# Five edits to a graph-network and feed-forward kernel: float16 counts, Gelus inside the attention, later source rows, other PSUM places, weight loads by another queue

## The chip, the cores and the metric

The kernel runs on one core of one Trainium2 chip. The metric is the device time of one execution in microseconds (us). Engines are named as the profile names them: PE (TensorE; PEld is its weight load), DVE (VectorE), ACT (ScalarE), POOL (GpSimd) and SP (SyncE, which here only issues DMAs). The sequencer of POOL issues DMAs too.

## The reference, cut to what matters

Four residual layers over 1250 nodes with 1024 features, and 20000 edges sorted by destination:

```
edge_index = stack([src, dst])
x = x + L0_gnn(layernorm(x), W, a_l, a_r, src, dst)     # attention over edges, 4 heads of 256
x = x + L0_ffn(layernorm(x), rail_maker, rail_up, w_cproj)   # small rails, exact gelu, @ w_cproj.T (16384 -> 1024)
x = x + L1_gnn(layernorm(x), edge_index, W, b)          # (x W.T + b), then a normalized sum over neighbours and self
x = x + L1_ffn(layernorm(x), shared + one of 8 experts by argmax)
```

In the attention, `e = leaky_relu(el[src] + er[dst])`, a softmax over the edges of each destination, and a sum of `alpha * z[src]`. The kernel turns the edge list into a dense matrix of counts (how often source n meets destination m), so that both graph layers become dense matrix products: the attention weight of a pair is its count times an exponential.

## The kernel before, in words

The nodes are cut into T = 10 tiles of R = 125. One function, gnn_ffn_kernel, writes all instructions; a scheduler orders those of each engine by their place in the program and by when their inputs are ready in its own model. `tc.issue_after(ins)` adds an edge: what the block issues on the engine of `ins` comes behind `ins`.

**Counts, L243 to L407.** The edges lie in 160 chunks of 125. For each chunk DVE makes two one-hot matrices in float16 (low_hot L286, place_hot L291), and PE multiplies them into counts in PSUM (count, L343). keep_counts (L297) copies a tile's counts to SBUF by ACT in float32 (cn) and stores them in DRAM (cnt_d) by SP. mark (L307) makes a table of -1e30 where a count is zero, for the search of the largest score. turn_counts (L312) transposes ten blocks of 125 x 125 per tile on PE (L318), and ACT copies them as int16 into CT (L321, L324). Beside it, a tile of x is normalized and transposed (L159), and z_tile (L232) makes Z for heads 0 and 1 (L228), copies it by ACT (L235) and sums el and er by DVE (L239). A fallback in tc.If counts all chunks when an edge lies outside its window; it does not run with these inputs.

**Second half of Z, L467 to L488.** For j = 0 to 19 heads 2 and 3 get their Z tiles. Beside it DVE searches the largest scores (maxima, L424), at j = 10 el_row(2) transposes head 2's el (L183), stores it to DRAM and spreads it to all partitions (L187, L192, both POOL DMAs), at j = 14 bounds makes the rows of heads 0 and 1, and at j = 16 the first three weights of head 0 are made ahead of that j's z_tile.

**Attention, L549 to L641.** attend(h, b) runs for four heads and two halves of the destinations. For each of ten source tiles weight (L455) makes an operand w: DVE (L458), ACT Exp (L459), DVE (L461, times the counts). PE adds w times Z into five PSUM accumulators po (L559). The last two source tiles are taken together, accumulator by accumulator. Then ACT copies the sums of the weights (L567), DVE inverts them (L568, in a group of two and a group of three) and adds to X (L571). Generators passed as `between` issue other work after each weight: the search for head 3 (els3, whose el_row stands ahead of the first attend) or first_half, which normalizes and transposes five tiles. After the last attend eight products of the rail matrices (hidden_rows, L541, four at a time over 32 rows) go through two PSUM buffers `pt` to ACT's Gelu (L639), and make the first blocks Y of the large product.

**Large product, L652 to L948.** The 16384 x 1024 product is cut into NB = 16 blocks of 49 steps (15 of seven by seven Strassen-like products, the last of another form). projection_plan (L54) writes the order of steps, and at which step each sum of X blocks (weights) and Y blocks (Gelu outputs) is issued to DVE (add_up, L721). A step is eight L728 matmul instructions; accumulate (L734) copies the result by ACT into one of five buffers (L737), and POOL sends it to DRAM with an adding DMA (L741); `sent` holds the last one. SP loads weights (load_weights, L516). In blocks 2 to 5 the GCN weights are prepared: at step 24 load_quarters (L751) issues four loads of 256 KB to four places taken from the free list of Y blocks, and at step 31 sum_quarters (L757) makes four sums on DVE (L759 to L762) behind the last add_up issued, and SP stores them (L764). Steps 28 and 30 hold the rails of the next block (L536).

**GCN product and aggregation, L950 to L1160.** linear (L975) multiplies by the prepared weights, the last result read from PSUM by L1030. Then Hs is split into a rounded part Hr (ACT, L1089) and the rest (DVE, L1091), and gather (L1105) multiplies each tile's counts with both (L1108) into PSUM tiles ph. load_counts (L1003) reads counts from cnt_d by POOL's queue into a float32r tile. logits uses PSUM tile pg, turn uses pt. The experts' layer (L1171 on) is not touched.

Of the kernel before, what the change touches and what calls it, by code (L numbers as in the profile page):

```python
# [102 lines left out]
def gnn_ffn_kernel(ctx, tc, x, src, dst, gat_w, a_l, a_r, maker, up, cproj,  # L103
# [14 lines left out]
    cnt_d = dram.tile([GS, R, LO], F32, name="cnt_d")  # L118
    cnt_t = cnt_d.rearrange("g m l -> (g m l)").rearrange("(c p t j) -> t p c j", c=T, p=R, t=T)
# [11 lines left out]
    make_identity(nc, ident)  # L131
    ones_row = const.tile([1, R], F32, name="ones_row")
# [75 lines left out]
    with tc.tile_pool(name="gw", bufs=1) as gwp, tc.tile_pool(name="gps", bufs=3, space=PSUM) as psp:  # L208
# [34 lines left out]
        with tc.tile_pool(name="cc", bufs=1) as ccp, tc.tile_pool(name="cw", bufs=2) as cwp:  # L243
# [10 lines left out]
            near = [[g for g in range(GS) if c in win[g]] for c in range(EC)]  # L254
            limit = ccp.tile([EP, EC], F32, name="limit")
# [41 lines left out]
            def keep_counts(d, parts):  # L297
                cn = cns[d] = cwp.tile([R, HI, LO], F32, name="cn")
                g0 = 0
                for i, pc in enumerate(parts):  # L300
                    n = pc.shape[-1] // LO
                    nc.scalar.activation(cn[:, g0:g0 + n].rearrange("p g l -> p (g l)"), pc, AF.Copy,
                                         accum_out=got[:, d, i % 3:i % 3 + 1])
                    g0 += n
                dma(nc.sync, cnt_d[d * HI:d * HI + HI].rearrange("g m l -> m g l"), cn)
# [6 lines left out]
            def turn_counts(d):  # L312
                cn = cns[d]
                CTv = CT.rearrange("p (h a) n -> p a h n", a=2)
                for blocks in ([(g, 0) for g in range(4)], [(g, 1) for g in range(4)], [(4, 0), (4, 1)]):
                    pt = psp.tile([R, 4, R], F32, name="pt")
                    for i, (g, a) in enumerate(blocks):
                        nc.tensor.transpose(pt[:, i, :], cn[:, g, a * R:(a + 1) * R], ident[:R, :R])  # L318
                    d0 = d * R + blocks[0][0] * GD
                    if len(blocks) == 4:  # L320
                        nc.scalar.copy(CTv[:, a, :, d0:d0 + 4 * GD],  # L321
                                       pt.rearrange("p g m -> p (g m)").rearrange("p (q h) -> p h q", h=HI))
# [69 lines left out]
            with tc.If(elsewhere > 0):  # L392
                with tc.tile_pool(name="hot2", bufs=1) as hotp:
                    for d in range(T):
# [11 lines left out]
                        keep_counts(d, parts)  # L406
# [48 lines left out]
        def weight(h, b, s):  # L455
# [3 lines left out]
            nc.scalar.activation(u, u, AF.Exp, bias=el2[:, h, s:s + 1])  # L459
# [5 lines left out]
        weighed = []  # L465

        with tc.tile_pool(name="mx0", bufs=1) as mxp:  # L467
            search = maxima({h: els0[:, h, :] for h in range(2)}, mxp)
            for j in range(2 * T):
                h, t = 2 + j // T, j % T  # L470
                if j == T:
# [5 lines left out]
                for _ in range(1 + j % 2 if j < T + 4 else 2):  # L477
                    next(search, None)
                if j == T + 6:
                    first_weights = [weight(0, 0, s) for s in range(3)]  # L480
                z_copied, z_summed = z_tile((h,), t, z_first[j][0] if j < 2 else None)
# [67 lines left out]
    with tc.tile_pool(name="aps", bufs=6, space=PSUM) as aps, tc.tile_pool(name="tps0", bufs=2, space=PSUM) as tps:  # L549

        def attend(h, b, between=iter(())):
# [963 lines left out]
```

## Time and profile before

| | us |
|---|---|
| runs: median (lowest, highest) | 2720.31 (2719.29, 2721.19) |
| profiled execution | 2725.58 |
| its span | 2723.9 |
| PE busy in the span | 2690.3 |
| DVE busy | 1662.9 |
| counts stage and first Z half | 0 to about 152 |
| second Z half | 152 to 230 |
| attention | 230 to 413 |
| large product | 419 to about 2210 |
| aggregation | 2350 to about 2462 |

A line of the list of waits has the engine, the tile and line that waited, the releaser, the total in us, how often, and the longest. A line of a stretch has its length, then busy us of PE, PEld, DVE, ACT and POOL with instruction counts, the TensorE clock that was granted (1.00 is full speed), the mean busy share of the 16 DMA engines and GB/s. A line of the timeline has start, duration, engine, line, operation, out<-in, shape, the number of instructions merged, and in brackets the idle time before it with its releaser. SPq and POOLq are the DMA issues of those engines. A matmul of float32 data is two instructions.

### The profile page before, as it was taken

What the parts mean: (1) busy time and instruction counts of PE and PEld (TensorE: products, weight loads), DVE (VectorE), ACT (ScalarE), POOL (GpSimd) and SP (SyncE); (2) the same over time, 40 slices, a digit from 0 to 9 for tenths busy, and PEclk for the clock granted to TensorE, in tenths of its full rate; (3) what the DMA queues carried; (4) which work ended last, traced back from release to release, by engine and by line L of the source; (5) the groups of instructions that cost most, each with busy time, mean ns of one, the idle gap of its engine ahead of it and who ended that gap; (6) DMA issues with size and microseconds to landing.
All of it is one profiled execution on the core that took longest, in us unless ns stands there. A gap on an engine that the chain in (4) does not pass through costs nothing. (4 is left out here: it accounts for less than half of the span.)

```text
span 2723.9 us, 32531 instructions
## 1 busy us (share of the span) xinstructions
PE 2690.3 (99%) x11285; PEld 1906.2 (70%) x11285; DVE 1662.9 (61%) x2884; ACT 949.3 (35%) x1689; POOL 765.8 (28%) x952
## 2 busy tenths in 40 slices
PE   8999999999999999999999999999999999999998
PEld 5678886676666766667667666676676764575797
DVE  9668988564656645655556465564655765532655
ACT  2333445434334343343443433434433011211232
POOL 2000001243333333433333333343333110012253
PEclk9999999999999999999999999999999999999999
DMA  6337216499999999999999999999999570342695
GB/s 188 93 85 182 71 39 220 165 199 164 222 195 184 233 175 194 187 163 204 179 172 201 162 195 182 167 202 172 157 211 268 151 126 12 74 91 85 217 291 170
DMA packets 267609, 452.63 MB, mean 166 GB/s; under 512 B 53382, under 2 KB 143662, under 8 KB 267053
## 3 DMA queue, kind: packets, MB, share of 16 engines
q0 software_dynamic: 126896, 278.80, 59.5%
q1 hardware_dynamic: 140532, 171.55, 21.0%
q8 instruction: 97, 1.59, 0.2%
q14 instruction: 84, 0.69, 0.1%
HBM read 180.57 MB, written 271.90 MB: 166 GB/s over the span
## 5 line engine op out<-in xcount | busy, mean ns | idle before, releaser
L741 POOL DMA_DIRECT2D acc_d<-low x686 | 590.4, 861 | 958.3 <-ACT low L737 907.1
L737 ACT COPY low<-po 128x626 f32<-128x626 f32 x735 | 501.1, 682 | 952.1 <-PE po L728 891.5
L728 PE MATMUL po<-X,arena 128*128 128x313 f32 x2200 | 619.0, 429 | 4.9 <-DVE X L721 4.9
L728 PEld LDWEIGHTS po<-X,arena 128*128 128x128 f32 x2200 | 414.9, 190 | 180.6 <-ACT low L737 16.0
L728 PE MATMUL po<-low,arena 128*128 128x313 f32 x1528 | 431.6, 428 | 0.0
L728 PEld LDWEIGHTS po<-low,arena 128*128 128x128 f32 x1528 | 287.1, 189 | 122.0 <-ACT low L737 11.6
L728 PE MATMUL po<-X,first_w 128*128 128x313 f32 x760 | 216.7, 428 | 0.0
L728 PE MATMUL po<-X,BZ 128*128 128x313 f32 x744 | 214.7, 432 | 0.0
L728 PEld LDWEIGHTS po<-X,first_w 128*128 128x128 f32 x760 | 142.6, 189 | 61.5 <-ACT low L737 7.6
L728 PEld LDWEIGHTS po<-X,BZ 128*128 128x128 f32 x744 | 141.3, 192 | 60.6 <-ACT low L737 5.8
L728 PE MATMUL po<-low,first_w 128*128 128x313 f32 x608 | 173.2, 427 | 0.0
L728 PEld LDWEIGHTS po<-low,first_w 128*128 128x128 f32 x608 | 114.5, 189 | 48.5 <-ACT low L737 4.4
L721 DVE TENSOR_TENSOR X<-X 128x626 f32<-128x626 f32 x125 | 100.4, 808 | 74.6 <-PE po L728 66.0
L228 PE MATMUL pz<-W,xT 128*125 128x256 f32 (+1 forms) x480 | 140.6, 451 | 0.9 <-ACT Z L235 0.6
L728 PE MATMUL po<-low,BZ 128*128 128x313 f32 x488 | 140.1, 427 | 0.0
L721 DVE TENSOR_TENSOR arena<-arena 128x512 f32<-128x512 f32 x126 | 86.5, 688 | 68.4 <-PE po L728 65.9
L721 DVE TENSOR_TENSOR X<-X,low 128x626 f32<-128x626 f32 x106 | 85.2, 807 | 56.6 <-PE po L728 46.4
L228 PEld LDWEIGHTS pz<-W,xT 128*125 128x125 f32 x480 | 88.7, 187 | 44.2 <-issue 33.8
L728 PEld LDWEIGHTS po<-low,BZ 128*128 128x128 f32 x488 | 91.5, 189 | 38.6 <-ACT low L737 3.7
L721 DVE TENSOR_TENSOR X<-low,X 128x626 f32<-128x626 f32 x100 | 80.2, 807 | 54.0 <-PE po L728 49.3
L713 ACT ACTIVATE X<-pz 128x626 f32<-128x626 f32 (+8 forms) x222 | 102.1, 523 | 18.3 <-PE pz L541 18.3
L721 DVE TENSOR_TENSOR low<-X 128x626 f32<-128x626 f32 x99 | 79.7, 808 | 38.3 <-PE po L728 31.1
(346 smaller groups left out, 3540.8 us busy)
## 6 DMA issues: line engine op xcount, KB each, us to landing
acc_d<-low POOLq DMA_DIRECT2D x735, 313.0 KB, 6.2
arena<-in_cproj SPq DMA_DIRECT2D x148, 256.0 KB
xT<-in_w SPq DMA_DIRECT2D x16, 1024.0 KB
BZ<-in_cproj SPq DMA_DIRECT2D x56, 256.0 KB
first_w<-in_cproj SPq DMA_DIRECT2D x52, 256.0 KB
w3t<-in_w SPq DMA_DIRECT2D x8, 1024.0 KB
low<-acc_d SPq DMA_DIRECT2D x20, 313.0 KB
X<-acc_d SPq DMA_DIRECT2D x18, 313.0 KB
```

What stands on the lines that cost most here:

```text
L228: made_z = nc.tensor.matmul(pz, xT[:, k, t * R:(t + 1) * R], W[hs[0] // 2][:, k, i:i + len(hs)], start=(k == 0), stop=(k == KD - 1))
L713: nc.scalar.activation(view(key)[:, :, n0 - n * NQ:n1 - n * NQ], pz[:, 2 * i:2 * i + 2, a + n0 - c0:a + n1 - c0], AF.Gelu)
L721: summed[:] = [tt(view(k), *a, op=ALU.add if sign == "+" else ALU.subtract).ins]
L728: nc.tensor.matmul(po[:, o, :NQ], view(x)[:, q, o * P:(o + 1) * P], view(y)[:, q, :], start=(i == q == 0), stop=(i + 1 == len(pairs) and q ...
L737: nc.scalar.copy(part, po[:, :, :NQ])
L741: sent[:] = [nc.gpsimd.dma_start(out=acc_d[p - 1, i - 1], in_=part, accum_op=ALU.add).ins]
```

## The change

- Counts are kept in float16 in SBUF and DRAM (keep_counts, mark, turn_counts, load_counts); the transposes of counts have float16 operands and output, with an identity of their own. In the fallback the old kind is kept and stored in a second DRAM tensor, all_d, as well.
- In the second half of Z, el_row(2) is issued one j later, and the first three weights come behind the z_tile of their j, with their ACT instructions behind that tile's copy.
- el_row(3) becomes a generator that the first attend runs after its third weight.
- The eight rail products and their Gelus are issued by a generator, in four pieces, inside the last source tiles of the last attend, with the Gelus behind the last Exp; that attend groups its accumulators three and two.
- The four GCN quarter loads go by POOL's queue, behind the last accumulation sent.
- PSUM tiles pg and pt of the aggregation are allocated ahead of ph, so that all three lie in other places.

```diff
+    cnt_d, all_d = (dram.tile([GS, R, LO], f, name=n) for f, n in ((F16, "cnt_d"), (F32, "all_d")))
...
+    ident16 = const.tile([R, R], F16, name="ident16")
+    nc.vector.tensor_copy(ident16, ident[:R, :R])
...
-            def keep_counts(d, parts):
-                cn = cns[d] = cwp.tile([R, HI, LO], F32, name="cn")
+            def keep_counts(d, parts, kind=F16):
+                cn = cns[d] = cwp.tile([R, HI, LO], kind, name="cn" if kind == F16 else "cn32")
...
             def turn_counts(d):
                 cn = cns[d]
+                i16 = cn.dtype == F16
...
                     pt = psp.tile([R, 4, R], F32, name="pt")
+                    pt = pt.rearrange("p g m -> p (g m)").bitcast(F16)[:, :4 * P].rearrange("p (g m) -> p g m", g=4)[:, :, :R] if i16 else pt
                     for i, (g, a) in enumerate(blocks):
-                        nc.tensor.transpose(pt[:, i, :], cn[:, g, a * R:(a + 1) * R], ident[:R, :R])
+                        nc.tensor.transpose(pt[:, i, :], cn[:, g, a * R:(a + 1) * R], ident16 if i16 else ident[:R, :R])
                     d0 = d * R + blocks[0][0] * GD
                     if len(blocks) == 4:
-                        nc.scalar.copy(CTv[:, a, :, d0:d0 + 4 * GD],
-                                       pt.rearrange("p g m -> p (g m)").rearrange("p (q h) -> p h q", h=HI))
+                        nc.scalar.copy(CTv[:, a, :, d0:d0 + 4 * GD].rearrange("p h (g q) -> p h g q", g=4),
+                                       pt.rearrange("p g (q h) -> p h g q", h=HI))
...
-            nc.scalar.activation(u, u, AF.Exp, bias=el2[:, h, s:s + 1])
+            raised[:] = [nc.scalar.activation(u, u, AF.Exp, bias=el2[:, h, s:s + 1]).ins]
...
-                if j == T:
+                if j == T + 1:
                     els2 = gwp.tile([P, KD, 2, F], F32, name="W", bufs=2)[:R].rearrange("p k h f -> p (k h f)")[:, :N]
                     el_row(2, els2, mxp, psp)
...
+                z_copied, z_summed = z_tile((h,), t, z_first[j][0] if j < 2 else None)
                 if j == T + 6:
-                    first_weights = [weight(0, 0, s) for s in range(3)]
-                z_copied, z_summed = z_tile((h,), t, z_first[j][0] if j < 2 else None)
+                    with tc.issue_after(z_copied.ins):
+                        first_weights = [weight(0, 0, s) for s in range(3)]
...
-        def attend(h, b, between=iter(())):
+        def attend(h, b, between=iter(()), inside=iter(()), first=2):
...
+                    if s == T - 1 and v < s and i != 2:
+                        next(inside, None)
                     nc.tensor.matmul(po[i], ws[v][:, i * R:(i + 1) * R], Z[h // 2][:, v, h % 2, :],
...
-            for group in (range(2), range(2, HT)):
+            for group in (range(first), range(first, HT)):
...
+            def fourth_row():
+                for _ in range(2):
+                    yield
+                el_row(3, els3, mxp, tps)
+
...
-            attend(0, 0)
+            attend(0, 0, fourth_row())
...
-            attend(3, 1, half)
-            for n in range(2):
-                for q in range(4):
...
+            def first_hidden():
+                for n in range(2):
+                    for i in range(2):
+                        buf[0, "Y", "11", f"{i + 1}{n + 1}"] = 2 * n + i
+                        for q in range(2):
+                            pz = tps.tile([P, 4, R], F32, name="pt").rearrange("p a b -> p (a b)")[:, :NQ]
+                            hidden_rows(pz, 0, n, 0, 2 * i + q)
+                            with tc.issue_after(raised[0]):
+                                nc.scalar.activation(YS[2 * n + i][:, q, :], pz, AF.Gelu)
+                        yield
+
+            pieces = first_hidden()
+            attend(3, 1, half, pieces, 3)
...
-                nc.sync.dma_start(quarter(i), gcn_w[(a + k) * P:(a + k + 1) * P, g * 512:(g + 1) * 512])
+                with tc.issue_after(sent[0]):
+                    nc.gpsimd.dma_start(quarter(i), gcn_w[(a + k) * P:(a + k + 1) * P, g * 512:(g + 1) * 512])
...
+        for name, n in (("pg", 1), ("pt", 2)):
+
+            psp.tile([P, 512], F32, name=name, bufs=n)
         pas = [psp.tile([R, 2, 512], F32, name="ph", bufs=2) for _ in range(2)]
```

More of the change, by code (lines that the diff above doesn't have):

```diff
@@ L117, in gnn_ffn_kernel @@
     x_t = x.rearrange("(t p) d -> t p d", p=R)
-    cnt_d = dram.tile([GS, R, LO], F32, name="cnt_d")
-    cnt_t = cnt_d.rearrange("g m l -> (g m l)").rearrange("(c p t j) -> t p c j", c=T, p=R, t=T)
+    cnt_d, all_d = (dram.tile([GS, R, LO], f, name=n) for f, n in ((F16, "cnt_d"), (F32, "all_d")))
+    cnt_t, all_t = (v.rearrange("g m l -> (g m l)").rearrange("(c p t j) -> t p c j", c=T, p=R, t=T) for v in (cnt_d, all_d))
     nm_d = dram.tile([GS, R, LO], BF16, name="nm_d")
@@ L254, in gnn_ffn_kernel @@
             near = [[g for g in range(GS) if c in win[g]] for c in range(EC)]
+            assert max(map(len, win)) * EP <= 2048
             limit = ccp.tile([EP, EC], F32, name="limit")
@@ L304, in keep_counts @@
                     g0 += n
+                if kind == F32:
+                    dma(nc.sync, all_d[d * HI:d * HI + HI].rearrange("g m l -> m g l"), cn)
+                    rounded = cwp.tile([R, HI, LO], F16, name="cn")
+                    nc.vector.tensor_copy(rounded, cn)
+                    cn = rounded
                 dma(nc.sync, cnt_d[d * HI:d * HI + HI].rearrange("g m l -> m g l"), cn)
@@ L405, in gnn_ffn_kernel @@
                                 nc.tensor.matmul(v, od[:, i * R:(i + 1) * R], os, start=(c == 0), stop=(c == EC - 1))
-                        keep_counts(d, parts)
+                        keep_counts(d, parts, F32)
                         mark(d)
@@ L463, in weight @@
             return w
-        weighed = []
+        weighed, raised = [], []
         with tc.tile_pool(name="mx0", bufs=1) as mxp:
@@ L574, in gnn_ffn_kernel @@
         with tc.tile_pool(name="mx1", bufs=1) as mxp:
-            els3 = el_row(3, elp.tile([R, 2, N], F32, name="els")[:, 0, :], mxp, tps)
+            els3 = elp.tile([R, 2, N], F32, name="els")[:, 0, :]
+            def fourth_row():
+                for _ in range(2):
+                    yield
+                el_row(3, els3, mxp, tps)
             search = maxima({3: els3}, mxp, [marks[:, t, :] for t in range(T)], 2)
-            attend(0, 0)
+            attend(0, 0, fourth_row())
             attend(0, 1, search)
@@ L632, in gnn_ffn_kernel @@
             attend(2, 1, half)
-            attend(3, 1, half)
-            for n in range(2):
-                for q in range(4):
-                    pz = tps.tile([P, 4, R], F32, name="pt").rearrange("p a b -> p (a b)")[:, :NQ]
-                    hidden_rows(pz, 0, n, 0, q)
-                    buf[0, "Y", "11", f"{q // 2 + 1}{n + 1}"] = 2 * n + q // 2
-                    nc.scalar.activation(YS[2 * n + q // 2][:, q % 2, :], pz, AF.Gelu)
+            def first_hidden():
[10 more added lines that the diff above has]
+            attend(3, 1, half, pieces, 3)
+            for _ in pieces:
+                pass
             for t in range(HT, T):
@@ L1134, in gnn_ffn_kernel @@
             for t in range(T):
-                nc.sync.dma_start(whole, cnt_t[t])
+                nc.sync.dma_start(whole, all_t[t])
                 tt(whole[:, t, :], whole[:, t, :], ident[:R, :R], op=ALU.add)
```

## The prediction, made before the changed kernel was run

> **What bounds the kernel now.** I read the page's busy shares first, then the list of who waited for whom on TensorE (PE), then stretches and the instructions in order of time around its largest waits.
>
> ```profile
> PE 2690.3 (99%) x11285; PEld 1906.2 (70%) x11285; DVE 1662.9 (61%) x2884; ACT 949.3 (35%) x1689; POOL 765.8 (28%) x952
> ```
>
> PE is busy for 2690.3 of 2723.9 us. The change removes no matmul, so it can win only idle time (33.6 us in all, of which the first 16 us and the last 24 us of the span, which it does not touch, hold most), time at a lower clock, and PE time of cheaper instructions. Who PE waited for (total, times, longest):
>
> ```profile
> PE po L728 <- DVE X L721: 4.9, 1, 4.9
> ...
> PE pt L183 <- DVE sc L239: 2.8, 2, 1.9
> ...
> PE pt L541 <- ACT X L639: 1.8, 3, 1.3
> ...
> PE ph L1108 <- ACT Hr L1089: 0.9, 1, 0.9
> ...
> PE pz L228 <- ACT Z L235: 0.6, 1, 0.6
> ```
>
> Each belongs to one part of the change. Two cost more than they show: in the stretches below (columns: length, busy of PE, PEld, DVE, ACT, POOL, then the granted clock), PE counts as busy at a clock of 0.50.
>
> ```profile
> 416.00:418.00 2.00, 1.50 (x7) 1.00 (x8) 1.97 (x5) 1.17 (x4) 0.00 (x0) 0.99 0.92 283
> 418.00:420.00 2.00, 2.00 (x6) 0.97 (x5) 1.65 (x4) 1.22 (x3) 0.00 (x0) 0.50 0.93 297
> ...
> 1045.00:1050.00 5.00, 2.11 (x10) 1.40 (x8) 0.89 (x2) 1.40 (x3) 1.72 (x2) 0.94 1.12 226
> 1050.00:1055.00 5.00, 3.01 (x6) 2.11 (x7) 5.00 (x8) 0.00 (x0) 0.00 (x0) 0.50 0.90 226
> ```
>
> So after a pause the clock stays at half for some microseconds. Sixteen matmuls of L728 take 7.12 us from 419.09 to 426.21 and 6.40 us from 1051.99 to 1058.39. At full clock eight take 2.11 us (starts at 1014.85 and 1016.96), so sixteen take 4.22. A pause alone does not do it: after 1.92 us at 191 us the clock was 1.00.
>
> **Part 1, GCN weights by GpSimd's queue.** The last quarter of the fourth group:
>
> ```profile
> 1034.06 0.33 SPq L755 DMA_DIRECT2D low<-in_gcn_w  x1
> ...
> 1049.11 0.69 DVE L760 TENSOR_TENSOR X<-low,X 128x512 f32<-128x512 f32 x1 [9.77 <-DMA low<-in_gcn_w]
> ...
> 1051.99 6.56 PE L728 MATMUL po<-X,arena 128*128 128x313 f32 x16 [4.88 <-DVE X L721]
> ```
>
> Issued at 1034.06, the load holds DVE until 1049.11, 15.05 us later; the sums for the next product (L721) stand behind L760, and PE waits 4.88 us. Price: 4.88 + (6.40 - 4.22) = **7.06 us**. PE ran dry at 1047.11 and restarts 2.88 us after DVE is released, so a release by 1044.23 costs nothing. Step 24 of the block starts at 1033.85 (four products and one rails step before the product at 1042.51): the limit is step 24 + 10.4 us. The third group agrees: release at 822.89, 9.3 us after its step 24, and no stall.
>
> The change issues all four loads behind the accumulation of step 22, which POOL starts at 1032.95 and which takes 0.86. Sixteen DMAs move. At 0.54 each (L830's median) the fourth starts near 1035.4, at 0.8 (its longest) near 1036.2: step 24 + 1.6 to 2.4. The fourth waits for a place that product 23 frees, at 1033.85, so POOL hardly stops for it. Behind it stand the accumulations of steps 23 and on, late by some 2 us; their ACT copies rotate over five buffers and a product takes 2.11 us, which covers it. How soon does it land? Nearest rows: the three gcn_w loads that POOL issues at 2093.6 to 2094.7, right behind accumulations, land after 7.7 us in the median; accumulations 4.4 to 9.2; SP's own fourth quarters 10.0 to 15.05. By 7.7 the release is at step 24 + 9.3 to 10.1: no stall. By 9.2 it is 0.4 to 1.2 us in each of four groups; by SP's rows see the rivals. I take the POOL rows and leave 1 us: gain **6.0** (bounds: 7.06 gain, 26 loss). In the first three groups SP issued the fourth load 2.3 to 4.0 us before step 24, so there the change only delays it; that is its danger.
>
> [...]
>
> **Part 2, the first Gelus inside the last attention.** From 412.76, when the last attention matmul ends, sixteen L541 matmuls and sixteen L728 matmuls take until 426.21: 13.45 us.
>
> ```profile
> 412.76 0.80 PE L541 MATMUL pt<-xT,BZ 32*128 32x313 f32 x4
> 414.83 1.11 PE L541 MATMUL pt<-xT,BZ 32*128 32x313 f32 x4 [1.28 <-ACT X L639]
> ...
> 419.09 7.29 PE L728 MATMUL po<-X,BZ 128*128 128x313 f32 x16
> ```
>
> Unhindered they need 16 x 0.0925 (eight in 0.74 at 429.81) + 4.22 = 5.70: **7.75 us** too much, through a Gelu table load (1.28) and PSUM that waits for ACT. ACT is free from 402.57 to 409.40, so with the change the table load and eight Gelus (0.38 each when two are back to back) lie beside the last twenty attention matmuls (4.35 us). Four pieces with two PSUM buffers: a pair of Gelus takes 0.76 and two semaphore steps, about 1.1 us, against 0.87 us of matmuls between pieces, so some 0.3 us is lost at each of two or three pieces. The L541 work still holds 1.5 us of PE. Taking three accumulators first (L565) frees the PSUM of the first product early. What is late next is DVE: its X-side sums need memory that the last matmul reads. Product 3 is due 4.2 us after that; three L571 (1.26), two weight sums (1.4) and a Y sum (0.81) are 3.5 us. If all four weight sums go first, as in the trace, PE waits about 1.4 us. Gain **5.8** (bounds 0 to 7.75).
>
> **Part 3, source rows later, weights after the Z copy.** Three waits go: 1.92 at 192.97 and 0.86 at 231.93 (the transpose L183 of a row whose last sum is not made), and 0.56 at 215.84 (Z's copy stood behind an Exp that waited for DVE until 214.7). Moved with each row are one transpose, one ACT copy (0.26) and two POOL DMAs (0.57 and 0.55); POOL is idle there. The second row comes one Z tile (3.45 us) later but PE arrives 1.92 earlier, so DVE, which already waited 4.00 us for it, gets it some 1.6 us later. DVE is busy nearly throughout from 203.7 to 233 and attention starts 2.5 us earlier: weight 3, made at 234.05 to 234.86 after 0.95 us of waiting for a buffer, is then wanted about 1.3 us before it is there. After that DVE needs 1.67 us per weight against PE's 2.2. 3.34 - 1.2 = **2.2** (bounds: 1 loss, 3.8 gain). The fourth row's spread (10.9 us to land) starts some 7 us later and its first user is 20 us away.
>
> **Part 4, counts in float16.** A hundred transposes (L318) change type. In each tile the first four wait for ACT's copies and hardly gain; six run in 0.73 us (103.63 to 104.36), 0.122 each. No float16 transpose is in the trace. Nearest row: float16 matmuls with the same weight shape and 250 columns (L343), 0.107 each; by columns alone half of that. So six to ten a tile gain 0.015 to 0.067 each: 1 to 6 us, and no loss, as the wider L343 is already faster. Weight loads are 140 ns against 187, a quarter less, and I take the same quarter: **2.5**. The marking pass (0.80 each, DVE) can only shorten; DVE has 8 us in 50 free there. The identity's copy (0.28, as L528) fits before 3.41, where DVE waits for a DMA; otherwise it costs 0.28. Count stores halve and count loads cast, but the loads (4.7 and 5.7 us to land) are issued three tiles of 10 us ahead.
>
> **Part 5, PSUM places.** PE's 0.93 us ends at 2350.26. The profile names ACT, but the first Hr copy was done at 2343.40; DVE's L1030, which reads the last product's PSUM, ends at 2350.06. With ph in other places the wait goes; the low parts (L1091) follow from 2349.97 and may hold PE 0.3 later. Gain **0.7** (0 to 0.93).
>
> **Sum.** 6.0 + 5.8 + 2.2 + 2.5 + 0.7 = 17.2 us. The profiled execution took 2725.58 (span 2723.9 and 1.7 around it), so 2708.4 in its own terms; it lies 5.3 above the median of the runs, 2720.31, and the stalls are not a matter of profiling that I can see, so the forecast is 2720.3 - 17.2 = **2703.1**.
>
> **Rivals.**
> - The end of attention trips the clock again: the pieces' small matmuls (32 rows, 313 columns) and DVE's lateness leave gaps. For it: 1.83 us of pauses sufficed before. Against: 1.92 in a dense stretch did not. Part 2 then gives about 1: 2708.
> - DVE limits attention: it is busy 48.55 of 50 us at 250 to 300. Part 3 gives nothing and two further stalls of 2 us come: 2709.
> - The loads land as SP's did before. With 10.0, 11.65, 11.5 and 15.05 us from step 24 + 1.4, the releases are 1.0, 2.7, 2.5 and 6.0 us past the limit; with 2.2 for the clock in the last that is 14.4 instead of 7.06. The other parts' 11.2 leave 2716; if each stall trips the clock, 2723: within 0.2%. [...]
> - Slower: four megabyte-sized bursts behind accumulations, in a stretch whose DMA engines are full, all land after 15 us. Each group stalls 6.0 + 2.2, 33 in all, 26 more than before: 2720.3 + 26 - 11.2 = 2735. A landing of about 13 us in all four (11 if each pause trips the clock) is where the sign turns. For it: 15.05 was seen. Against: no POOL transfer there took over 9.2.
> - An edit that does nothing, such as transposes at the old pace, lies in the forecast's range.
>
> **How the numbers follow.** Forecast 62%, clock again 13%, DVE-bound 8%, SP's landing 10%, slower 7%. Faster by over 0.2% (5.4 us, about what a measurement of this kernel can tell from no change): 62 + 13 + 8 = 83%; within: 10%; slower: 7%. Range: the bounds of parts 2 to 5 give 2695 below; above, the second rival with part 1 at half gives 2713, and the third rival's lower end 2716: 2694 to 2717.
>
> **What would show it.** L760 without a wait over 3 us and clock 1.00 near 1050; L728 at 0.264 a matmul right behind L559; no L183 wait; six L318 below 0.6 us; L1108 starting behind L982. Wrong would be DVE waits for in_gcn_w in several groups, POOL's accumulations pushing ACT's copies late, or PE waiting for w (L461) around 240.

## The result, and the profile after

The changed kernel takes 2713.64 us (median of 9 runs, 2712.15 to 2716.28) where the kernel before takes 2720.31 in the same comparison (9 runs, 2718.22 to 2728.58): a ratio of 0.9969, 95% interval 0.9959 to 0.9978, or 6.0 to 11.2 us less. The forecast was 2703.1, 17.2 us less. The sign was right, the gain less than half of it.

The profiled execution of the changed kernel has a span of 2710.8 us, 13.1 less than the profiled one of before, twice what the medians differ by. That is the first thing to explain. The page's busy shares, and then who waited for whom on PE (total, times, longest), both of the kernel after:

```profile
PE 2681.3 (99%) x11285; PEld 1898.2 (70%) x11285; DVE 1659.3 (61%) x2885; ACT 946.6 (35%) x1687; POOL 774.1 (29%) x968
```

```profile
PE po L574 <- DVE w L473: 3.1, 3, 1.5
PE pt L330 <- ACT cn L307: 2.4, 10, 0.3
PE po L759 <- issue: 2.1, 1, 2.1
...
PE ph L1140 <- ACT Hr L1121: 0.9, 1, 0.9
```

Of the five waits of before that the prediction shows, four have gone; the 0.9 us before the first ph matmul (L1140) is still there. Two have come instead: attention (L574) now waits for its weights from DVE, and the first projection matmul (L759) waits 2.1 us for something that the profile does not name ("issue").

In the group whose sums kept PE for 4.88 us before, at 1047 to 1052, the four quarter loads by GpSimd's queue (L787) now land in time. DVE waits 4.05 us, already at the first of its four sums (L791), which needs two of the loads; the last load lands 7.70 us after its issue, and DVE does not wait for it. PE's timeline there is without a bracket behind any matmul:

```profile
1029.41 0.54 POOL L787 DMA_DIRECT2D low<-in_gcn_w  x1
...
1036.61 0.69 DVE L791 TENSOR_TENSOR low<-X,low 128x512 f32<-128x512 f32 x1 [4.05 <-DMA X<-in_gcn_w]
...
1044.68 2.27 PE L759 MATMUL po<-low,first_w 128*128 128x313 f32 x8
1046.79 2.27 PE L759 MATMUL po<-low,arena 128*128 128x313 f32 x8
```

The end of the last attention (columns of the second view as before: length, busy PE, PEld, DVE, ACT, POOL, then the granted clock):

```profile
412.54 0.16 DVE L583 RECIPROCAL rs<-rs 125x2 f32<-125x2 f32 x1
412.62 0.67 DVE L752 TENSOR_TENSOR arena<-BZ 128x512 f32<-128x512 f32 x1
413.21 0.87 DVE L586 SCALAR_TENSOR_TENSOR X<-po,rs,X 125x256 f32<-125x256 f32 x2
...
414.18 6.14 PE L759 MATMUL po<-X,BZ 128*128 128x313 f32 x16 [2.12 <-issue]
```

```profile
412.00:414.00 2.00, 0.06 (x1) 0.00 (x0) 2.00 (x6) 0.17 (x1) 0.00 (x0) 1.00 0.89 272
414.00:416.00 2.00, 1.82 (x5) 1.33 (x6) 2.00 (x5) 0.00 (x0) 0.00 (x0) 0.70 0.96 320
416.00:418.00 2.00, 2.00 (x6) 1.26 (x5) 2.00 (x4) 0.00 (x0) 0.00 (x0) 0.50 0.91 283
```

The Gelus no longer stand in the way, but PE starts 0.1 us after DVE's last L586, which scales the last attention result and has a sum of 0.67 us (L752) ahead of it. That PE waited for this scaling is an inference, since the profile names nothing; the same 0.10 us lies between the two in all eight profiles that have the pause. The clock is then at half for 3.41 us, where the profile of before had 6.83. And the start of attention:

```profile
218.21 1.46 DVE L436 CUSTOM_DVE_ANT_0 sc<-nm,W 125x1250 f32<-125x1250 bf16 x1 [2.89 <-DMA nm<-nm_d]
...
221.13 1.46 DVE L436 CUSTOM_DVE_ANT_0 sc<-nm,W 125x1250 f32<-125x1250 bf16 x1 [1.11 <-DMA nm<-nm_d]
...
224.59 2.25 DVE L473 SCALAR_TENSOR_TENSOR w<-u,CT 125x625 f32<-125x625 f32 x3
225.54 6.74 PE L574 MATMUL po<-BZ,w 125*125 125x257 f32 x30 [1.55 <-DVE w L473]
```

The first three weights (L473) stand behind maxima (L436) that wait for a load of marks. ACT had finished their Exps at 217.6, so the order on DVE's queue makes them late, not their data.

### The profile page after: what moved, and what is told of

Same layout as the page of the kernel before. It is cut to its first block, busy times and chain, and to the rows that moved or that the text cites. A ratio compares the mean times of both kernels' runs of the same rounds, so it can differ in the third digit from the quotient of the medians.

```text
span 2710.8 us, 32556 instructions
## 1 busy us (share of the span) xinstructions
PE 2681.3 (99%) x11285; PEld 1898.2 (70%) x11285; DVE 1659.3 (61%) x2885; ACT 946.6 (35%) x1687; POOL 774.1 (29%) x968
## 5 line engine op out<-in xcount | busy, mean ns | idle before, releaser
L768 ACT COPY low<-po 128x626 f32<-128x626 f32 x735 | 500.4, 681 | 949.3 <-PE po L759 902.8
L759 PE MATMUL po<-X,arena 128*128 128x313 f32 x2200 | 616.3, 427 | 0.0
L759 PEld LDWEIGHTS po<-X,arena 128*128 128x128 f32 x2200 | 413.9, 189 | 174.1 <-ACT low L768 16.0
L759 PE MATMUL po<-low,arena 128*128 128x313 f32 x1528 | 431.7, 428 | 0.0
L759 PEld LDWEIGHTS po<-low,arena 128*128 128x128 f32 x1528 | 287.1, 189 | 121.5 <-ACT low L768 11.6
L759 PE MATMUL po<-X,first_w 128*128 128x313 f32 x760 | 216.7, 428 | 0.0
L759 PE MATMUL po<-X,BZ 128*128 128x313 f32 x744 | 213.5, 430 | 2.1 <-issue 2.1
L759 PEld LDWEIGHTS po<-X,first_w 128*128 128x128 f32 x760 | 142.6, 189 | 61.5 <-ACT low L768 7.6
L759 PEld LDWEIGHTS po<-X,BZ 128*128 128x128 f32 x744 | 140.6, 191 | 62.2 <-ACT low L768 5.8
L759 PE MATMUL po<-low,first_w 128*128 128x313 f32 x608 | 173.2, 427 | 0.0
L759 PEld LDWEIGHTS po<-low,first_w 128*128 128x128 f32 x608 | 114.5, 189 | 48.5 <-ACT low L768 4.4
L752 DVE TENSOR_TENSOR X<-X 128x626 f32<-128x626 f32 x125 | 100.4, 807 | 74.8 <-PE po L759 64.9
L759 PE MATMUL po<-low,BZ 128*128 128x313 f32 x488 | 140.3, 428 | 0.0
L752 DVE TENSOR_TENSOR arena<-arena 128x512 f32<-128x512 f32 x126 | 86.4, 687 | 67.9 <-PE po L759 64.5
L752 DVE TENSOR_TENSOR X<-X,low 128x626 f32<-128x626 f32 x106 | 85.2, 807 | 59.8 <-PE po L759 46.7
L759 PEld LDWEIGHTS po<-low,BZ 128*128 128x128 f32 x488 | 91.3, 189 | 39.2 <-ACT low L768 3.7
L752 DVE TENSOR_TENSOR X<-low,X 128x626 f32<-128x626 f32 x100 | 80.1, 806 | 57.5 <-PE po L759 50.0
L752 DVE TENSOR_TENSOR low<-X 128x626 f32<-128x626 f32 x99 | 79.8, 807 | 40.5 <-PE po L759 31.8
```

What stands on the lines that cost most here:

```text
L752: summed[:] = [tt(view(k), *a, op=ALU.add if sign == "+" else ALU.subtract).ins]
L759: nc.tensor.matmul(po[:, o, :NQ], view(x)[:, q, o * P:(o + 1) * P], view(y)[:, q, :], start=(i == q == 0), stop=(i + 1 == len(pairs) and q ...
L768: nc.scalar.copy(part, po[:, :, :NQ])
```

## The experiments

Fifteen runs follow, of twelve new kernels, once of the kernel before and twice of the changed one. Where an expectation speaks of sixteen products or of the sixteenth product, the first sixteen matmuls of the projection are meant, which are two products. To add up, each profile is cut into the same stretches (us, from the timelines; the ends of matmuls are modelled). "Z" is the time at which the second half of Z starts.

| kernel | Z | Z to attention | attention | to the end of 16 | to first ph |
|---|---|---|---|---|---|
| before | 151.7 | 78.7 | 182.5 | 13.5 | 1923.9 |
| before_again | 152.3 | 79.8 | 181.8 | 11.9 | 1918.5 |
| only_pool_queue | 152.1 | 79.4 | 181.4 | 14.5 | 1916.7 |
| only_psum | 152.4 | 78.8 | 182.3 | 14.5 | 1916.9 |
| only_f16 | 149.1 | 78.6 | 182.4 | 13.3 | 1920.4 |
| only_rows | 151.8 | 77.5 | 183.2 | 14.5 | 1923.6 |
| only_gelu | 151.8 | 78.9 | 189.5 | 9.6 | 1917.1 |
| all_but_pool_queue | 150.1 | 76.9 | 187.9 | 6.6 | 1916.8 |
| after | 148.9 | 76.7 | 186.5 | 8.3 | 1916.2 |
| after_again | 149.4 | 77.3 | 188.7 | 6.6 | 1916.2 |
| after_third | 148.6 | 77.1 | 187.6 | 6.6 | 1916.4 |
| sp_queue_later | 148.9 | 77.5 | 188.0 | 6.6 | 1916.2 |
| act_queue | 148.5 | 77.1 | 187.1 | 6.6 | 1918.6 |
| pieces_and_sums | 149.3 | 76.6 | 185.5 | 6.8 | 1916.6 |
| weights_sooner | 148.0 | 76.0 | 185.5 | 8.3 | 1916.2 |
| best | 149.3 | 76.0 | 183.6 | 6.8 | 1917.2 |
| own_pool | 148.8 | 75.9 | 183.6 | 6.8 | 1915.6 |

**Is the stall of part 1 always there?** The kernel before unchanged, part 1 alone, and all but part 1:

> The kernel before, unchanged, profiled once more. Theory A (the 7.06 us stall at 1047 to 1058 is an event of some executions): a run near 2719 to 2720 shows no PE wait for X at the end of the fourth GCN group, the last quarter load lands in 8 to 12 us instead of 15.05, and the run is about 5 to 7 us shorter than the 2725.58 of the first profiled execution. Theory B (the stall is in every execution): the load lands after 14 us or more again, PE waits about 4.9 us for X and 16 matmuls of L728 take about 6.4 us, at any time of the run.

```
# only_pool_queue: the one edit; all_but_pool_queue: the same edit taken out of the changed kernel
-                nc.sync.dma_start(quarter(i), gcn_w[...])
+                with tc.issue_after(sent[0]):
+                    nc.gpsimd.dma_start(quarter(i), gcn_w[...])
```

> The kernel before with part 1 alone (the quarter loads of the GCN weights by GpSimd's queue). Theory A (the stall is there in some executions only): the median falls by 0 to 1.5 us, and only the long ones among the times (2725 to 2729) go. Theory B (the stall is in every execution of the kernel before): the median falls by 6 to 7 us.

> The changed kernel with its quarter loads on SP's queue as before, so parts 2 to 5 alone. Theory A: nearly all of the whole change's 6.7 us is there, a median of 2713.5 to 2715, with some times 5 to 7 us above it. Theory B: parts 2 to 5 give 0 to 1 us, a median near 2720.

Measured beside 25 runs of before (median 2722.49, 2717.97 to 2731.97): before_again 2721.11 (ratio 0.9994, 0.9985 to 1.0004); only_pool_queue 2720.68 (2717.84 to 2722.06; 0.999, 0.9981 to 0.9999); all_but_pool_queue 2714.11 (0.9969, 0.9957 to 0.9982). Part 1 alone is worth 0.3 to 5.2 us by that interval, and the other parts make up the whole of the 0.9969. The kernel before itself came out 1.4 us below the 25 runs (before_again), and only_pool_queue lies only 0.4 below before_again, so by these times alone the gain of part 1 is hardly clear of the scatter. Theory A holds in the main. The profiled run of before_again, 2721.55, was 4.0 us shorter than the first, not 5 to 7, and among the six runs of all_but_pool_queue (2713.06 to 2715.60) the long times that theory A expected did not come. One correction: the stall does not simply come and go, it wanders between the four groups and changes its size. These lines are of before_again (second and fourth group) and of only_rows (first group), both with SP's queue:

```profile
824.98 0.69 DVE L760 TENSOR_TENSOR X<-X 128x512 f32<-128x512 f32 x1 [10.16 <-DMA X<-in_gcn_w]
827.86 2.35 PE L728 MATMUL po<-low,first_w 128*128 128x313 f32 x8 [1.64 <-DVE low L721]
...
1044.50 0.69 DVE L760 TENSOR_TENSOR X<-low,X 128x512 f32<-128x512 f32 x1 [7.72 <-DMA low<-in_gcn_w]
```

```profile
716.84 0.69 DVE L767 TENSOR_TENSOR X<-X 128x512 f32<-128x512 f32 x1 [10.57 <-DMA X<-in_gcn_w]
719.72 2.35 PE L735 MATMUL po<-X,arena 128*128 128x313 f32 x8 [2.49 <-DVE X L728]
```

The group at 1044.50 is the one that cost 7.06 us in the first profile; here its load is there after a wait of 7.72 and PE does not stop. Over the eight profiles with SP's queue DVE waits 5.73 to 10.57 us for the fourth quarter (32 groups), and PE stalls in 7 of the 32, by 0.28 to 4.88 us. Each of the seven is what the release lies past step 24 + 10.39 us, to 0.02. Over the eight with GpSimd's queue (32 groups) DVE waits 2.82 to 4.55 at the first sum, never for the fourth quarter, and PE never stalls for these sums. In the last column of the table SP's queue gives 1916.2 to 1923.9, median 1917.8, mean 1919.2; GpSimd's gives 1916.2 to 1917.2, median 1916.4, mean 1916.5, own_pool left out, which changes that stretch in another way. Part 1 is worth 1.4 us in the middle execution and 2.7 in the mean, and takes away the long ones.

**Queue or moment?** The changed kernel with the four loads issued by SP's queue or by ACT's, and the line that puts them behind the last accumulation kept. The expectations take it that the loads then go out behind the same accumulations. They do not: `issue_after` holds on the engine of `sent`, which is POOL, and the traces show the loads of SP and ACT going out earlier than GpSimd's.

```
                 with tc.issue_after(sent[0]):
-                    nc.gpsimd.dma_start(quarter(i), gcn_w[...])
+                    nc.sync.dma_start(quarter(i), gcn_w[...])      # act_queue: nc.scalar
```

> The changed kernel with its quarter loads issued behind the same accumulations, but by SP's queue. Theory Q (the queue decides): the fourth quarter's wait on DVE stays at 6 to 10 us as in all kernels with SP's queue, and PE waits for the sums behind it in one to four groups (0.3 to 5 us each); from the 16th product to the first ph matmul 1917 to 1930 us. Rival M (the moment decides, not the queue): DVE waits 2.8 to 4.1 us as in the kernels with GpSimd's queue, and that stretch stays at 1916.2 to 1916.7.

> The changed kernel with its quarter loads issued by ACT's queue, which carries no other load in this stretch. Theory Q1 (SP's loads are late because of what stands ahead of them on SP's queue): DVE waits 2 to 5 us for the fourth quarter, no PE wait. Rival Q2 (only GpSimd's queue is fast here, because the accumulating transfers of its own queue come to rest while it loads): DVE waits 6 to 10 us as with SP's queue, with PE waits of 0.3 to 5 us in some groups.

The fourth load by SP's queue (first fence, sp_queue_later) and by ACT's (second, act_queue), issue and release in the last group:

```profile
1024.07 0.33 SPq L787 DMA_DIRECT2D low<-in_gcn_w  x1
...
1028.10 6.49 PE L759 MATMUL po<-X,arena 128*128 128x313 f32 x24
...
1036.31 0.69 DVE L792 TENSOR_TENSOR X<-low,X 128x512 f32<-128x512 f32 x1 [8.11 <-DMA low<-in_gcn_w]
```

```profile
1025.65 0.33 ACTq L787 DMA_DIRECT2D low<-in_gcn_w  x1
...
1032.23 0.69 DVE L792 TENSOR_TENSOR X<-low,X 128x512 f32<-128x512 f32 x1 [3.40 <-DMA low<-in_gcn_w]
```

The matmul line is step 24 of the block. In sp_queue_later the four loads go out 13.7, 10.7, 8.3 and 4.0 us ahead of it, in every group, which is where all_but_pool_queue has them (its fourth once later): in effect it is that kernel again, and moment against queue is not decided by it. ACT's first three go out at about the same places as SP's, its fourth 1.2 to 3.1 us ahead of step 24; GpSimd's four go out from 0.3 us ahead to 2.1 behind, in one burst.

From the end of the fourth issue to the release it is 11.9 us by SP and 6.3 by ACT in the last group. Over the four groups SP has 10.6 to 11.9 and ACT 5.2 to 6.3; GpSimd's fourth loads land 6.6 to 7.2 after the end of their issue in the changed kernel. Between SP and ACT the queue decides: over all 32 groups SP's fourth load went out anywhere from 4.0 us ahead of step 24 to 0.2 behind and took 9.9 to 15.5 us from the start of its issue, and ACT's, from within that span, took 5.6 to 6.6. GpSimd's queue is not special: Q2 falls. How much of its own speed comes from the queue and how much from its later burst no run separates. On SP's queue the second and third quarter and four small loads (in_maker, in_up) are issued in the 7 us ahead of that fourth load; by ACT's queue those small loads stay on SP. That they are what holds it is likely, but no run isolates it. Theory Q's PE wait did not show in this one profile (1916.2), as it did not in 25 of the 32 groups. Q1's bound of 5 us for DVE's wait was a little short (3.40 to 6.04), and ACT's queue has a price of its own: PE waits 1.8 us for ACT's copies (L768) and the stretch is 1918.6.

**Each other part alone.** only_f16 has the counts and their transposes in float16; only_gelu the pieces inside attend(3, 1) with their Gelus behind raised[0]; only_rows the row at j == T + 1, the weights behind z_copied and the fourth row inside the first attention; only_psum the two reserving tiles "pg" and "pt". The lines of the diff that each has alone:

```
# only_f16
-                cn = cns[d] = cwp.tile([R, HI, LO], F32, name="cn")
+                cn = cns[d] = cwp.tile([R, HI, LO], kind, name="cn" if kind == F16 else "cn32")
...
+                        nc.tensor.transpose(pt[:, i, :], cn[:, g, a * R:(a + 1) * R], ident16 if i16 else ident[:R, :R])
# only_gelu
+                    if s == T - 1 and v < s and i != 2:
+                        next(inside, None)
...
+            attend(3, 1, half, pieces, 3)
# only_rows
-                if j == T:
+                if j == T + 1:
...
+                    with tc.issue_after(z_copied.ins):
+                        first_weights = [weight(0, 0, s) for s in range(3)]
...
+            attend(0, 0, fourth_row())
# only_psum
+        for name, n in (("pg", 1), ("pt", 2)):
+            psp.tile([P, 512], F32, name=name, bufs=n)
```

> The kernel before with part 4 alone (counts and their transposes in float16). From the two profiles: the second half of Z starts 2.5 to 3 us earlier than 151.67; six transposes in a row take 0.4 to 0.6 us against 0.73. If that carries through to the end, the median falls by 2.5 to 3 us. Rival: attention is limited by DVE or by the loads of the maxima, which do not come earlier, and PE gives part of it back behind 215: less than 1.5 us is left at 412.

> The kernel before with part 2 alone (first Gelus inside the last attention). Theory (from the profiles so far): from the end of the last attention matmul to the end of the first sixteen projection matmuls 6.6 to 8.3 us, against 11.9 to 14.5 in the four kernels without part 2; but the last attention is longer by four pieces of 0.73, 2.9 us in all; PE still waits about 2.1 us for DVE before the first product, and that wait may or may not halve the clock. Net 2.4 us with the clock halved in the profile and up to 4.5 without; median 2.5 to 4 us lower. The forecast's term was 5.8.

> The kernel before with part 3 alone (source rows turned later, first weights behind the copy of Z). Theory: the second half of Z takes 2 to 3 us less (76.7 against 78.7 to 79.8), but attention starts with waits for w of about 3 us in all where it had 0.8, since DVE makes the first three weights later; net 0 to 1 us in the profile and a median within 1 us of before. Rival: the forecast's 2.2 us, or more where the old pauses halved the clock (as at 194 in two profiles of the kernel before).

> The kernel before with part 5 alone (the sums of the aggregation in other PSUM places). Theory: PE still waits 0.9 us before the first ph matmul, until 0.2 us after the last DVE sum of the linear part, since the new places are given out only when that whole pool of PSUM is released; gain 0, median within 1 us of before. Rival (the forecast): the wait is gone, 0.7 us.

- only_f16: 2716.56 beside 2722.49, ratio 0.9981 (0.9968 to 0.9994). The interval holds the 2.5 to 3 us expected; the medians differ by 5.9. Z starts at 149.13; the gain is still there at the end of attention (410.06, against 412.8 to 413.9 in the four profiles with no part of the change ahead of that point). The rival falls. The last six transposes before the second half of Z, in the kernel before (first line) and in only_f16 (second), to be read by their start and that of the next matmul (151.55 and 149.01), 0.75 us against 0.44:

```profile
150.80 0.82 PE L318 MATMUL pt<-ident,cn 125*125 125x125 f32 x6
```

```profile
148.57 0.51 PE L330 MATMUL pt<-ident,cn 125*125 125x125 f16 x6
```

- only_gelu: 2718.74 beside 2721.86, ratio 0.9981 (0.9965 to 0.9997). The tail is 9.6 instead of 11.9 to 14.5, PE's 2.12 us wait is there, and the clock was halved for 6.83 us after it. Attention took 7 us longer in this profile, not 2.9: a pause of 2.51 at its start (the old L183 wait) halved the clock once more, for 3.41 us.
- only_rows: 2720.73 beside 2721.86, ratio 0.9991 (0.9979 to 1.0003), no change that can be measured. Z to attention is 1.5 shorter than the mean of the five kernels with neither part 2 nor part 3 (79.1), attention 1.1 longer; waits for w are 2.8 us, and the first, of 2.05, was followed by 3.41 us at half clock, which the 1.1 may owe to. Theory right in the main (the medians differ by 1.1 where at most 1 was expected).
- only_psum: one run, 2720.43. PE still waits 0.9 us before the first ph. Theory right as to the wait, its cause is tested below.

The medians of the four single parts that have more than one run add up to 12.0 us, more than the 6.7 of the whole change. Each interval is several us wide, so the sizes of the parts are taken from the stretches of the profiles, not from these times.

**The wait at the end of attention.** Two of the four pieces go behind the last attention matmul, and DVE's sums but the first, with the layer norm's statistics, behind its last L586:

```
-                    if s == T - 1 and v < s and i != 2:
+                    if s == T - 1 and v < s and i < 2:
...
-            attend(3, 1, half, pieces, 3)
+            attended = attend(3, 1, half, pieces, 3)
...
-                add_up(*sums[j][1:])
+                with tc.issue_after(attended.ins) if n < 8 and j > 0 else nullcontext():
+                    add_up(*sums[j][1:])
...
-                late_tile(late[m])
+                with tc.issue_after(attended.ins):
+                    late_tile(late[m])
```

> The changed kernel with two of the four hidden pieces behind the last attention matmul instead of inside, and with DVE's sums for the projection (but the first) and its layer norm statistics behind the last attention scaling L586. Theory (PE's 2.12 us pause before the first product is for the last L586, which stands behind a sum of 0.67 on DVE): the pause shrinks to below 0.3 us, filled with the two pieces (1.46 us); with the clock kept at 1.00 sixteen products take 4.2 us; from the last attention matmul to the end of the sixteenth product about 6 us with the attention 1.46 shorter; 2 to 4 us less than the changed kernel, median 2710 to 2712. Rival: what holds the first product is something else (the Gelus, PSUM), and the pause stays at 1.5 to 2 us; or DVE, with its sums moved behind, is now late for the third product, and PE waits there 1 to 2 us: median 2713 to 2714.

2712.05 (2710.45 to 2714.33) beside 2721.86: ratio 0.9961 (0.9948 to 0.9974). In its profile:

```profile
412.26 0.88 DVE L586 SCALAR_TENSOR_TENSOR X<-po,rs,X 125x256 f32<-125x256 f32 x2
412.66 1.11 PE L554 MATMUL pt<-xT,BZ 32*128 32x313 f32 x4 [0.52 <-ACT X L664]
...
413.70 4.49 PE L759 MATMUL po<-X,BZ 128*128 128x313 f32 x16
```

The pause of 2.12 is gone: the first product follows the last piece without a bracket, and DVE is not late for the next. Most of it was filled by the two pieces rather than shortened: the last L586 ends 1.7 us after the last attention matmul, where it was 2.0. A wait of 0.52 for a Gelu that frees PSUM is left. The size was just below what was expected (1.6 us less than the changed kernel's 2713.64, from another comparison, where 2 to 4 were), and the two ratios to the kernel before, 0.9961 and 0.9969, have intervals that overlap.

**The wait at the start of attention.** The last maxima go behind the first weights:

```
-                    next(search, None)
+                    with tc.issue_after(weighed[-1]) if weighed else nullcontext():
+                        next(search, None)
```

> The changed kernel with the last three maxima of the third head (L436) put behind the first three weights (L473) on DVE instead of ahead of them. Theory (in the changed kernel L473 stood at 224.59 although its Exps were done by 217.6, behind maxima that waited 2.89 and 1.11 us for nm): PE no longer waits 1.55 us for w at the start of attention nor 0.82 us for the fourth weight; first attention matmul 1 to 1.6 us earlier counted from the start of the second half of Z (76.7), end of the last attention matmul 2 to 2.4 us earlier; median 2711 to 2712. Rival: DVE has too much work in this stretch whatever its order; the maxima moved behind delay weights 4 to 6, the wait for w only moves to 231 to 240, and less than 1 us is won.

> The changed kernel with both corrections (two hidden pieces and DVE's sums behind the attention as in pieces_and_sums; the first weights ahead of the last maxima). If the two are independent: 2712.05 less 1.5 to 2.4, a median of 2709.5 to 2710.5, faster than both kernels. Rival: what is gained at the start of attention is lost at its end, where DVE is the later one: a median of 2711.5 to 2712.5.

weights_sooner 2711.38 beside 2721.8, ratio 0.9965 (0.9952 to 0.9978). PE's and DVE's timelines of it, to be held against 224.59 and 225.54 above:

```profile
224.00 6.76 PE L575 MATMUL po<-BZ,w 125*125 125x257 f32 x30 [0.46 <-ACT Z L239]
```

```profile
215.76 2.25 DVE L473 SCALAR_TENSOR_TENSOR w<-u,CT 125x625 f32<-125x625 f32 x3 [0.75 <-ACT u L471]
```

The weights are made at 215.76 and attention starts as soon as Z is copied. One wait for w of 0.8 is left, later. From the start of the second half of Z attention starts only 0.7 us earlier than in the profile after, where 1 to 1.6 were expected. best, with both corrections, takes **2708.24** (2707.02 to 2708.66; ratio 0.9953, 0.9940 to 0.9967), its longest run below the shortest of the changed kernel (2711.87, in another comparison); 5.4 us less by the medians, where the two corrections alone gave 1.6 and 2.3. By the ratios, which take out what differs between comparisons, it is 4.4, 2.2 and 1.1. Either way it is somewhat more than the sum of the two, which the theory did not expect. The rival falls.

**The wait before ph.** best with ph in a pool of its own, opened ahead of the release of the accumulators po:

```
         rest.close()
+        phst = ExitStack()
+        php = phst.enter_context(tc.tile_pool(name="php", bufs=2, space=PSUM, side="right"))
         accst.close()
...
-        for name, n in (("pg", 1), ("pt", 2)):
-            psp.tile([P, 512], F32, name=name, bufs=n)
-        pas = [psp.tile([R, 2, 512], F32, name="ph", bufs=2) for _ in range(2)]
+        pas = [php.tile([R, 2, 512], F32, name="ph", bufs=2) for _ in range(2)]
```

> The kernel best with the sums of the aggregation (ph) in a pool of their own, opened while the linear part's accumulators (po) are still held. Theory (the first ph matmul waits for the release of the whole pool of po, whose last reader on DVE ends 0.2 us before): the 0.9 us wait before the first ph matmul falls to 0.2 us or less, the stretch from the 16th product to the first ph matmul shrinks by 0.7 us, median 2707.5 or, within the scatter, equal to best's 2708.2. Rival: the wait is for ACT's casts (Hr) or the counts; it stays at 0.9 us.

**2707.02** (2706.50 to 2708.90), ratio 0.9945 (0.9932 to 0.9959). own_pool, with PE's first ph matmul and DVE's last sum of the linear part:

```profile
2330.70 2.43 PE L1145 MATMUL ph<-Hr,cs 125*125 125x512 f32 x8
2331.30 0.69 DVE L1065 TENSOR_TENSOR low<-low,po 125x512 f32<-125x512 f32 x1 [1.16 <-PE po L1017]
```

In the changed kernel these stood the other way round (DVE L1062 at 2335.64, first ph at 2336.54). The wait was for the release of po's whole pool, as the theory had it; other places for ph within the next pool do not touch it (only_psum). That those places were free of po follows from the order of the allocations; the traces show no addresses. The stretch is 0.6 shorter than in the changed kernel and 1.6 shorter than in best. How much of the 1.2 us between the medians of best and own_pool is this is not settled, since the two are not of one comparison.

**Program or execution?** The changed kernel twice more:

> The changed kernel, profiled again. Theory (whether a pause of 2 us halves the clock depends on when it falls, and changes between executions of one program): in one of these two further profiles at least the clock after PE's 2.12 us pause near 414 differs from the first profile's (0.50), with sixteen products in 4.2 to 4.5 us instead of 5.98; the median of all runs stays. Rival (the program decides): halved in both.

> As after_again: the changed kernel, a third profile. Theory: the clock after the 2.12 us pause may be 1.00 or 0.50. Rival: halved in all three.

The third profile:

```profile
415.41 4.46 PE L759 MATMUL po<-X,BZ 128*128 128x313 f32 x16 [2.12 <-issue]
```

The same pause of 2.12 us, and the same sixteen matmuls in 4.46 where the first profile has 6.14; in after_again 4.46 too. Theory right: of three executions of one program one had these matmuls behind the pause at a clock of 0.50, in 6.14, and two had them in 4.46. What decides it no run shows.

## Why the prediction was right or wrong

- **The base.** "The stalls are not a matter of profiling that I can see, so the forecast is 2720.3 - 17.2": this is the step that failed first. The profiled execution lay 5.3 us above the median, and it held the largest stall of PE in 32 groups (from the 16th matmul to the first ph it took 5.4 us longer than before_again); its whole price was subtracted from a median that hardly contained it. In its own terms (2725.58 - 17.2) the forecast was 2708.4; the profile after took 2712.61.
- **Part 1**, term 6.0, measured 1.4 (middle) to 2.7 (mean). The mechanism and the limit of step 24 + 10.4 us were right: no stall, and GpSimd's loads landed in 6.9 to 8.2 where 7.7 was taken. The size was that of one execution. That 7.7 fitted so well has some luck in it: the three loads behind it were the first of six issued in a row (L830), and the other three landed after 8.8 to 10.0, and "no POOL transfer there took over 9.2" holds for the accumulations alone. The group called the third in the prediction (release at 822.89) is the second of the four. Its sign "L760 without a wait over 3 us" came by the letter alone: that sum does not wait at all, but the one ahead of it does, 4.05 us, without harm to PE. The third rival, that the loads land as SP's do, did not come, and neither did the slower one. From the end of the fourth issue to the release it was 10.6 to 11.9 us by SP and 5.2 to 6.3 by ACT, for the same loads, issued 1 to 3 us apart: the issuing queue had its part in how soon a load landed.
- **Part 4**, term 2.5, measured 3.0: Z starts at 149.0 in the mean of eleven profiles with it, at 152.0 in the mean of six without. Six transposes in a row take 0.44 us in the changed kernel (148.31 to 148.75). Right.
- **Parts 2 and 3**, terms 5.8 + 2.2 = 8.0. From Z to the end of the sixteen matmuls it is 274.6 in the mean of five profiles with neither (before, before_again, only_pool_queue, only_psum, only_f16) and 271.6 in that of the six with both (after and its two repeats, all_but_pool_queue, sp_queue_later, act_queue): 3.1. In part 2 the failed step is "Taking three accumulators first (L565) frees the PSUM of the first product early", and with it "What is late next is DVE": DVE was named, but for the third product, with 1.4 us at worst. It was already late for the first, which starts 0.10 us behind the last scaling L586 in all eight profiles with the wait: 2.12 us, of which the sum ahead of that scaling is about 0.6. Why the first product needs the last scaling is open; a pool of PSUM released as a whole, as in part 5, would fit, but no run tests it here. Also, four pieces cost 0.73 each, 2.9 us of PE, where 1.5 was taken from eight matmuls in 0.74; the prediction's own line at 412.76 had four in 0.80. And the first rival (the clock trips again) came in three of the eight profiles that kept this 2.12 us wait. In part 3 the failed step is "3.34 - 1.2 = 2.2" (2.1, worked out again): only the fourth weight was taken as late. The first three were late as well, because the marks for the last maxima were, and they stood behind them. With those two orders mended (best), Z to the end of the sixteen takes 266.4 in its one profile, which no half clock disturbs there, 8.2 less than with neither part: the forecast's 8.0 was there to be had, but not in this program.
- **Part 5**, term 0.7, measured 0. The failed step is "with ph in other places the wait goes". The place was not what the wait was for; own_pool shows what was.

The sum from the parts is 3.0 + 3.1 + 1.4 to 2.7 + 0 = 7.5 to 8.8 us, within the interval of 6.0 to 11.2.

## What to carry to other kernels

A stall in one profile is a sample: before its price is subtracted, see whether the profiled run lies off the median of the runs, and if it does by about that price, take a second profile. Where a wait is removed, read the engine that releases next in the order of its queue: the loss at the start of attention, and part of the one at its end, came from instructions that were ready but stood behind others that were not due. A wait for PSUM can be for the release of a pool rather than of a place, and then moving the tile within the next pool does nothing (0.9 us before the first ph in only_psum as in before, 0.2 in own_pool).

## What the runs showed of the hardware

The granted clock after a pause of PE, from 140 to 1200 us in all 17 profiles: none of nine pauses of 1.37 to 1.93 us was followed by a half clock, ten of eighteen of 1.97 to 2.51 were, one of 3.47 (only_f16, at 1047.52) was not, and one of 4.88 was. Behind the 2.12 us pause a halving cost 1.7 us (after against after_third) to 3.1 (only_gelu, tail of 9.6 against 6.6).

The length of the pause does not tell these cases apart: the 2.12 us pause was followed by a clock of 0.50 from 414.78 to 418.20 in after, for 3.41 us, and by 1.00 up to 420 in after_third. Two stretches of each, one after the other, around that pause (columns as before):

```profile
411.37:414.78 3.41, 1.29 (x6) 0.74 (x5) 2.96 (x7) 0.58 (x3) 0.00 (x0) 1.00 0.92 298
414.78:418.20 3.42, 3.42 (x8) 2.31 (x7) 3.42 (x6) 0.01 (x1) 0.00 (x0) 0.50 0.91 290
```

```profile
410.65:414.07 3.42, 2.65 (x12) 1.36 (x11) 2.61 (x7) 1.67 (x6) 0.00 (x0) 1.00 0.70 219
414.07:417.48 3.41, 2.07 (x8) 1.58 (x9) 3.41 (x7) 0.00 (x0) 0.00 (x0) 1.00 0.91 296
```

In after the pause lies within the first stretch, of which PE is idle for 0.62; in after_third it lies across the two, which are idle for 0.22 and 0.39. In before the clock was 0.50 for 6.83 us from 417.96, where the longest pause ahead of it, among the small matmuls of the hidden layer, is 1.28 us. What decides whether the clock is halved is not shown by these runs.

A piece of four hidden-layer matmuls (32 rows, 313 columns) held PE for 0.73 us, as long as eight of them in a row (0.74 in the profile of before). By the source a piece lies on two groups of 32 rows and the eight on four; no run tests whether this is the reason. Here the cut into four pieces had a price, 2.9 us of PE for sixteen matmuls that take 1.5 at the pace of the eight, though each piece fits between other matmuls.
